# A two-layer graph kernel: exponentials with a constant scale and a bias tile, a fourteenth pair weighted on GpSimd, and a re-ordered way into the main loop

## The chip, the cores and the metric

The kernel runs on one core of one Trainium2 chip. The metric is the time of one execution on the device in microseconds (us). Three runs of the kernel before gave 10816.57, 10823.91 and 10828.75 us, so the median is 10823.91 us.

## The reference

There are 3327 nodes with 128 features, a 0/1 adjacency matrix `adj` of 3327 x 3327, and two residual layers.

```python
# layer 0
h   = relu(layernorm(x))
deg = adj.sum(axis=1); deg[deg == 0] = 1
agg = adj.T @ h / deg
x   = x + relu(batchnorm(agg @ W_n.T + b_n + h @ W_c.T + b_c))
# layer 1: 128 independent attentions of 3327 x 3327, each with 8 columns
h = relu(layernorm(x))
q, k, v = (h @ W.T).reshape(128, 3327, 8) for W in (Wq, Wk, Wv)
a = softmax(q @ k.T / sqrt(128) + adj + adj, axis=2)
x = x + (a @ v).reshape(3327, 1024) @ Wo.T
```

Nearly all of the work is the middle of layer 1: 128 score matrices of 3327 x 3327, each of which is formed, has the adjacency added twice, goes through an exponential and is multiplied by `v` with a column of ones appended, which gives the softmax's sums.

## The kernel before, in words

**Scores and their exponentials.** `HALF` is half of 1/sqrt(128), so exp(q.k/sqrt(128) + 2 adj) = exp(2 (HALF q.k + adj)). The score is kept transposed: its 3327 rows, padded to 3328, are split into 26 chunks (`NC`) of 128 partitions, and its columns into 7 blocks of 512 (`NB`), the last of 255. Four of the 128 attentions (`G`) are handled together, which gives 32 groups (`NG`); two of them make a "half". A *pair* is one chunk and one half: a tile of 128 x 2 x 512 scores, held in two PSUM banks. A block of one group has 26 x 2 = 52 pairs.

**The main loop** (`attention`, lines 592 to 794) is written out: 32 groups x 7 blocks x 13 steps (`SU`), 2912 steps of four pairs each. Three of the four are *plain*: TensorE forms the score (`product`, L662), VectorE adds the adjacency into one third of the tile `d` (`add`, L753), and ScalarE later takes one exponential of all three, 128 x 3072, in place (`late`, L781). The fourth is *weighted*: ScalarE takes the exponential straight from PSUM into the tile `f` (L761), and GpSimd multiplies it by exp(2 adj), which was worked out beforehand and lies in the DRAM tensor `wd` (L762). Pairs 0 to 38 of a block are plain and 39 to 51 weighted, so the weighted ones touch chunks 19 to 25 (`WC` = 19). TensorE then multiplies each exponential by `v` into the accumulator `av` (`weigh`, L546).

**Order.** The scheduler is off, so each engine runs its instructions in the order in which the program writes them. Step x writes: the weighted product, its exponential and its multiplication; `late`, the exponential of `d` of step x-1; plain product 0 and its add; `second(0)`, the first four `av` matmuls of step x-2 (`LAG` = 2); one part of `finish`; `beside`, one part of a projection or of an output; plain products 1 and 2 with their adds; `second(1)`, the other four `av` matmuls. Products share three PSUM tiles in turn (pool `psc`), and every step uses four. `finish` divides a block's accumulator by its sums: a VectorE copy (L554) in step 2 of the next block, four transposes (L561) in step 3, reciprocal and multiplication on VectorE (L567, L569) in step 4, a store in step 5. `beside` runs the projections that later groups need in steps 6 to 11.

**Ahead of the loop.** Layer 0 loads `x` and its weights, normalises, and passes the 26 row chunks of `adj` (tile `a`, three buffers, loads at L396) through seven PSUM accumulators (L398). After that come the degree scaling (`spread`), the two small matmuls and the batch norm (`hidden`, L446 to L457), and a bound on the largest exponent (L463 to L485), which yields `flag` and the tile `scales`. If the bound is too large, `scales` is zero, so that nothing overflows, and a slow branch redoes layer 1. `weigh_early` (L422) takes the exponentials of three adjacency blocks for `wd`; the fourth and later ones are made inside the loop (L686). Layer 1's norm goes chunk group by chunk group: `relu`, `residual`, `stats`, `second_norm` (a normalise on ScalarE), `columns` (transpose and copy). `project_now` makes the projections of the first two groups, `loads` fetches the first group's q, k and v, and a sort on GpSimd (L175) puts k in order.

Of the kernel before, what the change touches and what calls it, by code (L numbers as in the profile page):

```python
# [20 lines left out]
H = 8  # L21
# [10 lines left out]
WC = 3 * SU // 2  # L32
# [12 lines left out]
def tile_two_layer_gnn(  # L45
# [60 lines left out]
    scales = const.tile([P, 2], F32, name="scales")  # L106
# [31 lines left out]
    def loads(tiles, d):  # L138
# [12 lines left out]
        qs = [dma(*a) for b in range(G) for a in q_loads(q, 32 * b, batch(b))]  # L151
# [9 lines left out]
        for half in range(2):  # L161

# [7 lines left out]
            todo += [qs.pop(0) for _ in range(2)]  # L170
            for c in range(0, NC, 4):
                n = min(4, NC - c)

                def sort(ks=ks, c=c, n=n, half=half):
                    nc.gpsimd.tensor_copy(  # L175
                        k[:, c : c + n, half * 64 : half * 64 + 64],
                        ks.bitcast(F32).rearrange("g (p c) -> g c p", c=NC)[:, c : c + n, :],
                    )

                todo.append(sort)  # L180
                if qs:
                    todo.append(qs.pop(0))
# [90 lines left out]
    with tc.tile_pool(name="l0", bufs=1) as l0, tc.tile_pool(  # L273
# [21 lines left out]
        for c0, c1 in ((0, 8), (8, NC - 1)):  # L295
            nc.sync.dma_start(xs[:, c0:c1, :], xr[:, c0:c1, :])
# [18 lines left out]
        def stats(i):  # L315
# [5 lines left out]
            cs = slice(4 * i, min(NC, 4 * i + 4))  # L321
            nc.scalar.activation(sd[:, cs], mv[:, cs, 1], AF.Sqrt, bias=eps)

        def normalise(i, dst):

            cs = slice(4 * i, min(NC, 4 * i + 4))
            nc.vector.reciprocal(rs[:, cs], sd[:, cs])
            nc.vector.scalar_tensor_tensor(
                mr[:, cs], mv[:, cs, 0], -1.0, rs[:, cs], ALU.mult, ALU.mult
            )  # L330
# [91 lines left out]
        def weigh_early():  # L422
            a7, n0, w = weights.pop(0)
            nc.scalar.activation(a7[:, :, :w], a7[:, :, :w], AF.Exp, scale=scales[:, 0:1])
            nc.sync.dma_start(
                wd[:, :, n0 : n0 + w].rearrange("c p n -> p c n"), a7[:, :, :w]
            )

# [13 lines left out]
        for i, (n0, w) in enumerate(blocks):  # L442
            if i == NQ - 1:
                spread(i)
# [3 lines left out]
            if i >= 1:  # L448
                hidden(i - 1)
        hidden(NQ - 1)  # L450
        nc.vector.bn_aggr(bmv, bst.rearrange("p i s -> p (i s)"))
        nc.scalar.activation(scale, bmv[:, 1:2], AF.Sqrt, bias=eps)
# [5 lines left out]

        top = l0.tile([P, 1], F32, name="top")
        nc.vector.tensor_reduce(top, amax, AX.X, ALU.max)  # L463
        nc.tensor.transpose(aside[:1, :P], top, ident)
        bound = l0.tile([1, 2], F32, name="bound")
        big = l0.tile([1, 2], F32, name="big")
        for i in range(2):
            nc.vector.tensor_tensor(
                big[:, i : i + 1], norm[:, 2 * i : 2 * i + 1], norm[:, 2 * i + 1 : 2 * i + 2],
                ALU.max,  # L470
            )
        nc.vector.tensor_tensor(bound[:, 1:2], big[:, 0:1], big[:, 1:2], ALU.mult)
        nc.vector.tensor_scalar(
            bound[:, 1:2], bound[:, 1:2], (1.001 * D * H * HALF) ** 2, 1e10,
            ALU.mult, ALU.min,
        )
        nc.scalar.activation(bound[:, 1:2], bound[:, 1:2], AF.Sqrt)
        nc.vector.tensor_reduce(bound[:, 0:1], aside[:1, :P], AX.X, ALU.max)
        nc.vector.tensor_tensor(bound[:, 0:1], bound[:, 0:1], bound[:, 1:2], ALU.add)
        nc.vector.tensor_scalar(bound[:, 0:1], bound[:, 0:1], SAFE / 2, None, ALU.is_le)  # L480
        nc.vector.tensor_scalar(flag, bound[:, 0:1], -1.0, 1.0, ALU.mult, ALU.add)
        for i, f in enumerate((2.0, 2.0 * HALF)):
            nc.vector.tensor_scalar(big[:, i : i + 1], bound[:, 0:1], f, None, ALU.mult)
        nc.tensor.matmul(aside[:, :2], ones[:1, :P], big, start=True, stop=True)
        nc.vector.tensor_copy(scales, aside[:, :2])  # L485

        weigh_early()
# [13 lines left out]
        def second_norm(i):  # L501
            normalise(i, C)

        def columns(i):
            pt, cs = turned(i, C, acc[i])
            (nc.vector.tensor_copy if i % 2 else nc.scalar.copy)(B[:, cs, :], pt)
            nc.sync.dma_start(hd[:, 4 * i * P : (4 * i + pt.shape[1]) * P], B[:, cs, :])

        wk = sp
# [3 lines left out]
        def project_now(j, banks):  # L513
            todo = projections(wk, B2[:, j * CH : (j + 1) * CH], j, True, ov0)
# [6 lines left out]
        for i in range(NQ):  # L521
            relu(i)
            residual(i)
            stats(i)
            if i >= 1:
                second_norm(i - 1)
                columns(i - 1)
            if i == 1:
                project_now(0, [acc[j] for j in (2, 3, 4, 5, 6)] + [aside])
                first = loads(sets[0], 0)  # L530
                for start in first[:13]:
                    start()
                weigh_early()
            if i == 3:
                for start in first[13:]:
                    start()
        second_norm(NQ - 1)
        columns(NQ - 1)
# [12 lines left out]
    def finish(rp, av, d0, n0, w):  # L551
# [15 lines left out]
        nc.vector.reciprocal(ri[:R, :, :J], pv[:R, :, :J, H])  # L567
# [24 lines left out]
    def attention():  # L592


        with tc.tile_pool(name="adj", bufs=4) as ap, tc.tile_pool(
# [17 lines left out]
            if True:  # L613
# [8 lines left out]
                def pairs(s):  # L622

                    three = [(j // 2, j % 2) for j in range(3 * s, 3 * s + 3)]
                    j = 3 * SU + s
# [363 lines left out]
```

## Time and profile before

| | |
|---|---|
| median of three runs | 10823.91 us |
| the profiled execution: time, span of its instructions | 10826.13 us, 10824.3 us |
| granted TensorE clock over the execution | 0.994 of full |
| adjacency pass of layer 0, first to last matmul | 20.6 to 187.0 us |
| first exponential of the main loop | 291.1 us |
| end of the last exponential of the main loop | 10803.2 us |
| DMA: bytes moved, mean rate | 1786.09 MB, 165 GB/s |

Busy time is the time in which an engine executes, whatever its rate. A group of instructions is given by line, engine, operation and tiles, with its count, busy time and the mean duration of one, and then the idle time of the engine just before them with what ended it. Successive instructions of an engine may overlap, so durations can add up to more than busy time. In the timeline each row has its start, its length and its count, and in brackets the idle time before it.

### The profile page before, as it was taken

What the parts mean: (1) busy time and instruction counts of PE and PEld (TensorE: products, weight loads), DVE (VectorE), ACT (ScalarE), POOL (GpSimd) and SP (SyncE); (2) the same over time, 40 slices, a digit from 0 to 9 for tenths busy, and PEclk for the clock granted to TensorE, in tenths of its full rate; (3) what the DMA queues carried; (4) which work ended last, traced back from release to release, by engine and by line L of the source; (5) the groups of instructions that cost most, each with busy time, mean ns of one, the idle gap of its engine ahead of it and who ended that gap; (6) DMA issues with size and microseconds to landing.
All of it is one profiled execution on the core that took longest, in us unless ns stands there. A gap on an engine that the chain in (4) does not pass through costs nothing. (4 is left out here: it accounts for less than half of the span.)

```text
span 10824.3 us, 186291 instructions
## 1 busy us (share of the span) xinstructions
PE 9805.0 (91%) x72399; PEld 2707.2 (25%) x72399; DVE 9915.9 (92%) x9936; ACT 10472.1 (97%) x6009; POOL 7001.0 (65%) x3640
## 2 busy tenths in 40 slices
PE   7899999999999999999999999999999999999998
PEld 3222222222222222222222222222222222222222
DVE  5899999999999999999999999999999999999998
ACT  5999999999999999999999999999999999999999
POOL 1566666666666666666666666666666666666665
PEclk8999999999999999999999999999999999999999
DMA  7655555555555555555555555555555555555554
GB/s 243 211 170 160 162 160 168 164 163 161 159 160 171 164 161 161 160 165 167 163 162 162 160 167 163 165 162 159 158 171 163 162 162 157 163 169 162 158 153 127
DMA packets 1145405, 1786.09 MB, mean 165 GB/s; under 512 B 198430, under 2 KB 446236, under 8 KB 1137084
## 3 DMA queue, kind: packets, MB, share of 16 engines
q1 hardware_dynamic: 1141982, 1771.79, 54.2%
q8 instruction: 568, 9.31, 0.4%
q14 instruction: 329, 2.70, 0.1%
q10 hardware_dynamic: 2494, 2.30, 0.1%
q0 software_dynamic: 32, 0.00, 0.0%
HBM read 1673.22 MB, written 100.53 MB: 164 GB/s over the span
## 5 line engine op out<-in xcount | busy, mean ns | idle before, releaser
L753 DVE SCALAR_TENSOR_TENSOR d<-s,at 128x1024 f32<-128x1024 f32 x8736 | 9454.2, 1141 | 746.9 <-PE s L662 711.5
L762 POOL TENSOR_TENSOR f<-f,wt 128x1024 f32<-128x1024 f32 x2912 | 6500.9, 2232 | 3529.7 <-ACT f L761 3526.0
L781 ACT ACTIVATE d<-d,scales 128x3072 f32<-128x3072 f32 x2912 | 7784.4, 2673 | 20.6 <-DVE d L753 1.0
L546 PE MATMUL av<-d,v 128*9 128x512 f32 x34944 | 5707.1, 565 | 560.0 <-ACT d L781 559.4
L662 PE MATMUL s<-q,k 32*128 32x512 f32 x23296 | 4106.5, 479 | 377.3 <-DVE d L753 294.0
L761 ACT ACTIVATE f<-s,scales 128x1024 f32<-128x1024 f32 x2912 | 3049.8, 1047 | 169.5 <-PE s L662 152.9
L662 PEld LDWEIGHTS s<-q,k 32*128 32x128 f32 x23296 | 1668.7, 181 | 5492.7 <-DVE d L753 3460.9
L546 PE MATMUL av<-f,v 128*9 128x512 f32 x11648 | 2834.0, 565 | 0.0
L546 PEld LDWEIGHTS av<-d,v 128*9 128x9 f32 x34944 | 653.7, 88 | 2016.2 <-ACT d L781 1223.9
L175 POOL CAST k<-ks 128x256 fp32r<-128x256 f32 (+1 forms) x448 | 286.8, 642 | 61.9 <-DMA ks<-kT 41.3
L546 PEld LDWEIGHTS av<-f,v 128*9 128x9 f32 x11648 | 307.1, 88 | 0.0
L398 PE MATMUL acc<-a,A 128*128 128x512 f32 (+1 forms) x364 | 151.7, 569 | 20.6 <-DMA a<-in_adj 20.6
L561 PEld LDWEIGHTS av<-ident,avs 128*128 128x128 f32 (+1 forms) x864 | 121.0, 208 | 179.3 <-issue 178.2
L561 PE MATMUL av<-ident,avs 128*128 128x128 f32 (+1 forms) x864 | 163.5, 310 | 0.5 <-DVE avs L554 0.5
L215 POOL TENSOR_TENSOR o<-pf,o 104x512 fp32r<-104x512 f32 x120 | 154.3, 1286 | 9.6
L554 DVE COPY avs<-av 128x512 f32<-128x512 f32 (+1 forms) x224 | 144.0, 643 | 2.8 <-PE av L546 2.8
L405 DVE TENSOR_REDUCE amax<-a 128x1 f32<-128x3327 f32 x26 | 93.7, 3611 | 40.7 <-DMA a<-in_adj 40.7
L398 PEld LDWEIGHTS acc<-a,A 128*128 128x128 f32 x364 | 69.0, 192 | 105.5 <-issue 105.3
L402 ACT ACTIVATE junk<-a 128x3327 bf16<-128x3327 f32 x26 | 77.4, 2977 | 6.7 <-DMA a<-in_adj 6.5
L213 DVE COPY pf<-av 104x512 f32<-104x512 f32 x120 | 81.7, 681 | 0.0
L371 POOL TENSOR_TENSOR sq<-wk 128x512 f32<-128x512 f32 x2 | 2.1, 1040 | 112.6 <-PE aside L372 112.6
L214 POOL CAST o<-pf 104x512 fp32r<-104x512 f32 x120 | 73.6, 614 | 0.0
(107 smaller groups left out, 899.8 us busy)
## 6 DMA issues: line engine op xcount, KB each, us to landing
at<-in_adjT SPq DMA_DIRECT2D x1920, 512.0 KB
wt<-wd SPq DMA_DIRECT2D x1344, 256.0 KB
at<-in_adjT SPq DMA_DIRECT2D x320, 255.0 KB
ks<-kT SPq DMA_DIRECT2D x512, 104.0 KB
q<-qT SPq DMA_DIRECT2D x512, 104.0 KB
a<-in_adj SPq DMA_DIRECT2D x26, 1663.5 KB
wt<-wd SPq DMA_DIRECT2D x224, 127.5 KB
qT<-o SPq DMA_DIRECT2D x128, 208.0 KB
```

The costliest lines, as they stand in the source:

```text
L175: nc.gpsimd.tensor_copy(k[:, c : c + n, half * 64 : half * 64 + 64], ks.bitcast(F32).rearrange("g (p c) -> g c p", c=NC)[:, c : c + n, :],)
L215: nc.gpsimd.tensor_tensor(o[:CH, 1], f[:CH], o[:CH, 0].bitcast(F32), ALU.subtract)
L398: nc.tensor.matmul(acc[i][:, :w], A[:, c, :], a[:, n0 : n0 + w], start=(c == 0), stop=(c == NC - 1),)
L405: nc.vector.tensor_reduce(amax[:, c : c + 1], a[:, :N], AX.X, ALU.max, apply_absolute_value=True)
L546: nc.tensor.matmul(av[32 * b : 32 * b + H + 1, :w], tiles[2][:, b, c, :], e, start=first, stop=last,)
L554: nc.vector.tensor_copy(avs[:, :w], av[:, :w])
L561: nc.tensor.transpose(pt[:R, j, :], avs[:, j : j + (R - 1) * J + 1 : J], ident)
L662: nc.tensor.matmul(p[:, x, :we], k[rs, c, :], q[rs, n0 : n0 + we], start=True, stop=True,)
L753: nc.vector.scalar_tensor_tensor(d[:, j, :, :w], p[:, :, :w], HALF, have[0, i, y, c // 2][:, c % 2, :w] .unsqueeze(1).to_broadcast([P, 2, w]),
L761: nc.scalar.activation(f[:, :, :w], p[:, :, :w], AF.Exp, scale=scales[:, 1:2])
L762: nc.gpsimd.tensor_tensor(f[:, :, :w], f[:, :, :w], have[1, i, y, ps[3][0]][:, :w].unsqueeze(1).to_broadcast([P, 2, w]), ALU.mult,)
L781: nc.scalar.activation(flat, flat, AF.Exp, scale=scales[:, 0:1])
```

## The change

Six things are done.

1. All exponentials take `scale=2.0` (or `2.0 * HALF`) as a constant and the tile `low` as a bias, where before they took `scales` as a scale and no bias. `low` is 0 when the bound holds and -1e30 otherwise. The bound is worked out without a square root, and ahead of the batch norm.
2. Step 12 of every block has two plain and two weighted pairs, so pairs 0 to 37 are plain and 14 are weighted. `WC` stays 19; the last adjacency tile of a block is loaded with one chunk instead of two.
3. `finish` takes the maximum of the sums and 1e-30 ahead of the reciprocal.
4. `x` is loaded from ScalarE's queue instead of SP's, so the first adjacency loads lead SP's queue.
5. Two of the three `weigh_early` calls move to the batch norm's loop; the last group's `spread` moves ahead of it.
6. Layer 1's norm: chunk group 0 by itself, then one square root, one reciprocal and one product for all others; normalise on VectorE and GpSimd instead of ScalarE; the relu in `columns`; one store of `hd`. The first group's q loads go out from ScalarE's queue, ahead of the rest, all loads at once, and three of every seven sorts of k run on VectorE.

```diff
-WC = 3 * SU // 2
+WC = 19
...
-            nc.sync.dma_start(xs[:, c0:c1, :], xr[:, c0:c1, :])
+            nc.scalar.dma_start(xs[:, c0:c1, :], xr[:, c0:c1, :])
...
-            nc.scalar.activation(a7[:, :, :w], a7[:, :, :w], AF.Exp, scale=scales[:, 0:1])
+            nc.scalar.activation(a7[:, :, :w], a7[:, :, :w], AF.Exp, bias=low, scale=2.0)
...
-            if i == NQ - 1:
-                spread(i)
             s = slice(n0, n0 + w)
             nc.vector.tensor_tensor(B2[:, s], acc[i][:, :w], B2[:, s], ALU.mult)
             nc.tensor.matmul(acc[i][:, :w], wn, B2[:, s], start=True, stop=True)
             if i >= 1:
                 hidden(i - 1)
+            if i in (3, 6):
+                weigh_early()
...
-        for i in range(NQ):
-            relu(i)
-            residual(i)
-            stats(i)
-            if i >= 1:
-                second_norm(i - 1)
-                columns(i - 1)
-            if i == 1:
-                project_now(0, [acc[j] for j in (2, 3, 4, 5, 6)] + [aside])
-                first = loads(sets[0], 0)
-                for start in first[:13]:
-                    start()
-                weigh_early()
-            if i == 3:
-                for start in first[13:]:
-                    start()
-        second_norm(NQ - 1)
-        columns(NQ - 1)
+        relu(0)
+        residual(0)
+        relu(1)
+        stats(0, False)
+        relu(2)
+        roots(0, 4)
+        residual(1)
+        factors(0, 4)
+        second_norm(0, nc.vector)
+        columns(0, True)
+        relu(3)
+        stats(1, False)
+        residual(2)
+        project_now(0, [acc[j] for j in (6, 5, 4, 0)] + [aside, acc[1]])
+        first = loads(sets[0], 0, True)
+        for start in first:
+            start()
+        for i in range(4, NQ):
+            relu(i)
+        for i in range(2, NQ):
+            if i > 2:
+                residual(i)
+            stats(i, False)
+        roots(4, NC)
+        factors(4, NC)
+        for i in range(1, NQ):
+            second_norm(i, nc.gpsimd if i % 3 == 0 else nc.vector)
+        for i in range(1, NQ):
+            columns(i, i % 2 == 0)
+        keep_columns(0, NQ)
         project_now(1, [acc[j] for j in (0, 1, 2, 3, 4, 5)])
         weigh_early()
...
-        nc.vector.reciprocal(ri[:R, :, :J], pv[:R, :, :J, H])
+
+        nc.vector.tensor_scalar(ri[:R, :, :J], pv[:R, :, :J, H], 1e-30, None, ALU.max)
+        nc.vector.reciprocal(ri[:R, :, :J], ri[:R, :, :J])
...
-                    three = [(j // 2, j % 2) for j in range(3 * s, 3 * s + 3)]
-                    j = 3 * SU + s
-                    return three + [(j // 2, j % 2)]
+
+                    last = s == SU - 1
+                    plain = [(j // 2, j % 2) for j in range(3 * s, 3 * s + 3 - last)]
+                    rest = [(WC + s // 2, 1 - s % 2)]
+                    return plain, rest + ([(NC - 1, 0)] if last else [])
...
-                    p = product(i, y, *ps[3])
-                    nc.scalar.activation(f[:, :, :w], p[:, :, :w], AF.Exp, scale=scales[:, 1:2])
...
+                    def weighted(c, half):
+                        f = fp.tile([P, 2, NB], F32, name="f")
+                        p = product(i, y, c, half)
+                        nc.scalar.activation(
+                            f[:, :, :w], p[:, :, :w], AF.Exp, bias=low, scale=2.0 * HALF
+                        )
+                        nc.gpsimd.tensor_tensor(
+                            f[:, :, :w], f[:, :, :w],
+                            have[1, i, y, c][:, :w].unsqueeze(1).to_broadcast([P, 2, w]),
+                            ALU.mult,
+                        )
+                        es.append(f)
+
+                    weighted(*rest[0])
                     if late is not None:
                         late()
-                    add(0, product(i, y, *ps[0]))
+                    add(0, product(i, y, *plain[0]))
                     if due:
                         second(0)
                     step()
                     beside(i, y, s)
-                    add(1, product(i, y, *ps[1]))
-                    add(2, product(i, y, *ps[2]))
+                    add(1, product(i, y, *plain[1]))
+                    if len(rest) > 1:
+                        weighted(*rest[1])
+                    else:
+                        add(2, product(i, y, *plain[2]))
...
-                        nc.scalar.activation(flat, flat, AF.Exp, scale=scales[:, 0:1])
+                    def late(d=d, w=w, n=len(plain)):
+                        flat = d[:, :n].rearrange("p j x n -> p (j x) n")[:, :, :w]
+                        nc.scalar.activation(flat, flat, AF.Exp, bias=low, scale=2.0)
```

## The prediction

> **What bounds the kernel now.** I read the busy table first, then ScalarE's groups by shape, then the waits, then single steps of the timeline.
>
> The page's busy table (busy us, share of the span, instructions):
>
> ```profile
> span 10824.3 us, 186291 instructions
> PE 9805.0 (91%) x72399; PEld 2707.2 (25%) x72399; DVE 9915.9 (92%) x9936; ACT 10472.1 (97%) x6009; POOL 7001.0 (65%) x3640
> ```
>
> ScalarE (ACT) leads, and most of its idle time is not in the loop. The same by stages (ahead of the loop, the loop, after it; columns: length, then busy us and count of PE, PEld, DVE, ACT, POOL):
>
> ```profile
> 212.00:291.00 79.00, 34.45 (x82) 15.45 (x82) 25.04 (x90) 35.41 (x58) 9.02 (x17) 0.59 0.75 218
> 291.00:10803.00 10512.00, 9587.74 (x71831) 2605.56 (x71831) 9764.08 (x9678) 10328.08 (x5840) 6970.92 (x3587) 1.00 0.54 163
> ```
>
> In the loop ScalarE is idle for 10512 - 10328 = 184 us of 10512: it sets the pace. Its groups by shape (busy us, mean ns of one, idle before):
>
> ```profile
> L781 ACT ACTIVATE d<-d,scales 128x3072 f32<-128x3072 f32 x2496 | 7133.0, 2858 | 19.9 <-DVE d L753 0.3
> L761 ACT ACTIVATE f<-s,scales 128x1024 f32<-128x1024 f32 x2496 | 2763.3, 1107 | 123.6 <-PE s L662 107.2 <-POOL k L175 7.3 <-issue 6.8
> L781 ACT ACTIVATE d<-d,scales 128x1530 f32<-128x1530 f32 x416 | 651.4, 1566 | 0.7 <-DVE d L753 0.7
> L761 ACT ACTIVATE f<-s,scales 128x510 f32<-128x510 f32 x416 | 286.5, 689 | 45.8 <-PE s L662 45.7
> ...
> L364 ACT ACTIVATE C<-aside,bias 128x512 f32<-128x512 f32 x6 | 4.1, 688 | 17.1 <-PE aside L361 17.1
> ...
> L452 ACT ACTIVATE bn_scale<-bn_mv,eps 128x1 f32<-128x1 f32 x1 | 0.3, 294 | 3.1 <-DVE bn_mv L451 3.1
> L477 ACT ACTIVATE bound<-bound 1x1 f32<-1x1 f32 x1 | 0.2, 202 | 1.4 <-DVE bound L473 1.4
> ```
>
> Successive exponentials overlap: over the 2496 full steps, the median from the start of `f` to that of `d` is 1.00 us and from `d` to the next `f` 2.75 us, so an undisturbed step takes 3.74 us. VectorE's three adds take 3.49 us (below): it follows closely, and is late where it has more to do. That is step 4 of a block, where `finish` divides; here are ScalarE's and VectorE's timelines in one such step (start, length):
>
> ```profile
> 361.00 2.85 ACT L781 ACTIVATE d<-d,scales 128x3072 f32<-128x3072 f32 x1
> 363.75 1.10 ACT L761 ACTIVATE f<-s,scales 128x1024 f32<-128x1024 f32 x1
> 364.85 2.86 ACT L781 ACTIVATE d<-d,scales 128x3072 f32<-128x3072 f32 x1
> ```
>
> ```profile
> 358.51 3.49 DVE L753 SCALAR_TENSOR_TENSOR d<-s,at 128x1024 f32<-128x1024 f32 x3 [0.70 <-PE s L662]
> 361.92 0.25 DVE L567 RECIPROCAL ri<-av 128x16 f32<-128x16 f32 x1
> 362.20 0.29 DVE L569 TENSOR_TENSOR oq<-av,ri 128x128 f32<-128x128 f32 x1
> ```
>
> The last `d` starts at the end of `f` (364.85), not 0.10 us ahead of it. Over the 150 full blocks that follow a full one (from the third group on), the `d` of step 4 starts 93 to 94 ns after the step's third add, from the 5th to the 95th percentile; in steps 0 and 1 it starts some 0.71 us after it. So in step 4 VectorE sets ScalarE's pace.
>
> **1. Constant scale, bias tile: 0.** What matters is how many per-partition operands an exponential reads. Without one, the 1x1 square root L477 took 202 ns; with a bias tile, L452 took 294: an operand costs 92 ns. Before, each exponential has a scale tile; after, a bias tile. From PSUM, L364 with a bias tile took 688 ns for 512 columns, L761 with a scale tile 689 for 510: equal within 3 ns. 5,824 of them at 3 ns would be 17 us; I take 0. If the tile were free: -5,824 x 92 ns = -536 us, and ScalarE's step of 3.74 - 0.18 = 3.56 us would still be longer than VectorE's 3.49, so that is the lower end.
>
> **2. The fourteenth pair: +32 us.** ScalarE's elements stay the same, but step 12 has three exponentials instead of two. `d` of 3072 becomes 2048: the slope between its two forms is (2858 - 1566)/(3072 - 1530) = 0.838 ns, so 0.858 us go. A second `f` comes, 1.00 us from start to start. Net +0.14 us x 192 full blocks = 27; short blocks 0.589 - 0.427 = +0.16 x 32 = 5. VectorE loses 224 adds (1.16 us each between starts), GpSimd gains 224 multiplications of 2.39 us:
>
> ```profile
> L762 POOL TENSOR_TENSOR f<-f,wt 128x1024 f32<-128x1024 f32 x2496 | 5967.4, 2391 | 3146.9 <-ACT f L761 3143.1 <-DMA wt<-wd 3.7
> ```
>
> GpSimd waits 3147 us for `f`, and the result is used two steps later, so its added 0.5 ms is hidden; if that cover failed, 224 x 2.39 = 535 us. VectorE's gap in step 12 brings nothing, I think: its lead is bounded by the three PSUM tiles, and by the products behind `second`, which waits for ScalarE's `d`. In steps 0 and 1 it is already 0.71 us ahead, and the losses come later: in step 3 TensorE's four transposes hold the adds up again. Bounds: 10 (a short block's steps are partly TensorE's) to 45.
>
> The Trainium skill (GPSIMD Engine Reference, section 4.1) speaks against the move: two-input elementwise work is about 2x slower on GpSimd than on VectorE. The rows agree on the rate (2391 against 1217 ns) but show a waiting GpSimd; by the rule, with 1.17 us more on the path of 224 blocks, the sum would be 262 us higher.
>
> **3. The maximum in `finish`: +42 us.** One VectorE instruction on 128x16 from PSUM, like the reciprocal it precedes (0.25 us, 0.28 to the next start); the reciprocal then reads SBUF and waits for it, like the 128x4 ones at 0.16 us, so 0.17 and 0.21 to the next start. Step 4 has 0.28 + 0.21 - 0.28 = 0.20 us more. VectorE being last there, it passes through to `d`: 160 blocks, 32 short ones (also 94 ns) and about half of the 31 first blocks of a group, some 208 x 0.20 = 42. What is queued behind it on VectorE is adds 1 and 2 of that step; who waits is `d`. Bounds: 0 (a lead from step 12 reaches step 4) to 60 (0.27 us each, as for a second PSUM read).
>
> **4. Adjacency first: +4 us.** The adjacency pass is TensorE's (busy 164.9 of 166.4 us), so only its start at 20.6 us counts. Before, ScalarE had its first chunk of `A` at 14.4 us and the pass waited for `a`. Now two `a` loads run beside `x`, which comes later than 10 us; ScalarE's queue issues the other loads in order, and in the built program some of those issues wait for the landing of `x` and of both `a`. `x`, `a`, `a` are 5.1 MB; at the 283 GB/s of the first 20 us they land at 18 to 20 us; four more issues at 0.4 us, table load 1.3, square root 0.5, factors 1.1 make 23 to 26. At 400 GB/s it would be 19. Bounds -3 to +15.
>
> **5. Bound and early exponentials moved: -3 us.** They leave the path behind the batch norm (208.3 to 211.5 us), but the bound and the last `spread` now stand ahead of the first B product in VectorE's and TensorE's queues (187.2 becomes about 192). The relu that starts layer 1 moves from 211.5 to about 208.5. Two of six activation table loads go, 1.30 us each here (231.67 to 232.97). By the Trainium skill (ScalarE: Activation LUTs, section "What ACT_TABLE_LOAD costs") a switch is about 2.66 us with its drain; no such drain stands in this trace; by the page two more us or so would go.
>
> **6. Layer 1's norm: -1 us.** ScalarE loses 22 normalises of 0.4 us and six square roots, but its queue now holds 16 q issues (about 0.6 us each where seven stood on SP), some waiting for earlier transfers, ahead of relu 4 to 6. VectorE's sorts of k's second half stand ahead of `stats(2)`; they wait for loads that can only start when the first half's buffer is sorted, about 12 us in all (before, first sort 242.3, second half landed 267.0). Counted through, VectorE is free at about 247 to 250 instead of stepping along; 8 us of residuals and stats, 9 of normalise and columns follow: `columns` ends at 264 to 268 against 269.5. From there the path is as before: project, exponential, its store must land (290.9), loop. Bounds -20 to +20.
>
> **Sum:** 0 + 32 + 42 + 4 - 3 - 1 = +74 on the profiled execution's 10826.1, less some 5 for short blocks in which TensorE, not ScalarE, is last: 10895. The profiled execution lies 2.2 above the median: **10893 us, 0.64% slower**.
>
> **Rivals.** A measurement here can tell about 0.2% (22 us) from no change.
> - *The bias tile is cheaper than the scale tile* (the other side). Place: 5,824 exponentials; price up to 92 ns each; above 12 ns each it outweighs the +69 and from 16 ns the kernel is faster by over 0.2%. At full price 10893 - 536 = 10357, or somewhat more, as VectorE's 3.49 us then leaves little room. Against it: 688 and 689 ns. Chance 8%.
> - *Step 12's free VectorE time carries into steps 2 to 5.* Then the maximum costs nothing and part of the 39 us that steps 3 and 5 of full blocks now take beyond 3.74 us each comes back: 10893 - 42 - (0 to 39) = 10812 to 10851. For it: 1.16 us freed. Against: the 0.71 us bound. Chance 20%.
> - *The way in gets longer*: ScalarE blocked on q issues, VectorE on sorts: +25, 10920. Chance 14%. *Or shorter* by 25: 10868. Chance 12%.
> - Forecast (10875 to 10910): 43%. Something else: 3%.
>
> Faster: 8%, the lower end of the second rival 4, other 2: 14%. Same: the rest of that rival's lower half and the lowest shorter way in, 16%. Slower: 70%. The range 10805 to 10945 takes in the second rival and both ways in; it leaves out the cheap tile and tails.
>
> **What would show it.** Right: `d` and `f` keep their durations (2858, 1107) with `low`; `d` of 2048 takes about 2.0 us; step 12 plus step 0 last 0.14 us longer; `d` of step 4 starts 94 ns after its add and 0.2 us later; the loop, 291 to 10803 before, is 60 to 80 us longer. Wrong: shorter exponentials; or slack at step 4; or a first `f` 20 us off 291.

## The result, and the profile after

The changed kernel takes 10925.59 us (median of four runs, 10920.39 to 10928.46), the kernel before 10823.62 in four runs beside it: a ratio of 1.0094, 95% interval 1.0077 to 1.0112. So it is 0.94% slower, by 102 us. The prediction was 10893 us (slower, 70%) with a range of 10805 to 10945. The profiled execution took 10925.71 us, its span is 10924.0 us, 99.7 longer than before.

The page's busy table (busy us, share of the span, instructions):

```profile
span 10924.0 us, 186996 instructions
...
PE 9819.1 (90%) x72399; PEld 2713.0 (25%) x72399; DVE 9738.8 (89%) x9955; ACT 10492.5 (96%) x6201; POOL 7481.9 (68%) x3864
```

VectorE has 177 us less work than before, GpSimd 481 more, ScalarE 20 more. The same by stages, ahead of the loop and in it (length, then busy us and count of PE, PEld, DVE, ACT, POOL; then clock, DMA share, GB/s):

```profile
212.00:298.70 86.70, 24.50 (x82) 14.63 (x82) 32.12 (x106) 16.98 (x23) 9.99 (x17) 0.60 0.64 160
298.70:10902.50 10603.80, 9611.36 (x71831) 2611.97 (x71831) 9580.15 (x9677) 10363.21 (x6064) 7450.44 (x3811) 1.00 0.53 157
```

The loop took 10512 us before and takes 10604, and ScalarE's idle time in it rose from 184 to 241 us. The stretch from 212 us to the loop went from 79 to 86.7 us. ScalarE's groups by shape (busy us, mean ns of one, idle before):

```profile
L832 ACT ACTIVATE d<-d,low 128x3072 f32<-128x3072 f32 x2304 | 6587.3, 2859 | 50.6 <-DVE d L794 31.2
L804 ACT ACTIVATE f<-s,low 128x1024 f32<-128x1024 f32 x2688 | 2967.9, 1111 | 144.6 <-PE s L703 130.0 <-POOL k L181 7.9 <-DMA wd<-a 6.7
L832 ACT ACTIVATE d<-d,low 128x1530 f32<-128x1530 f32 x384 | 601.5, 1566 | 6.2 <-DVE d L794 6.2
L832 ACT ACTIVATE d<-d,low 128x2048 f32<-128x2048 f32 x192 | 386.8, 2015 | 0.0
```

The durations with a bias tile are those with a scale tile (2858, 1107, 1566), and the `d` of two pairs takes 2015 ns. What is new is the end of the first line: `d` waits for VectorE's adds, 31.2 us in all against 0.3. That is step 4 of a block. ScalarE and VectorE there, in the block that the prediction showed (start, length):

```profile
369.17 2.85 ACT L832 ACTIVATE d<-d,low 128x3072 f32<-128x3072 f32 x1
371.92 1.10 ACT L804 ACTIVATE f<-s,low 128x1024 f32<-128x1024 f32 x1
373.22 2.86 ACT L832 ACTIVATE d<-d,low 128x3072 f32<-128x3072 f32 x1 [0.20 <-DVE d L794]
```

```profile
370.09 0.16 DVE L604 TENSOR_SCALAR ri<-av 128x16 f32<-128x16 f32 x1
370.29 0.25 DVE L605 RECIPROCAL ri<-ri 128x16 f32<-128x16 f32 x1
370.57 0.29 DVE L607 TENSOR_TENSOR oq<-av,ri 128x128 f32<-128x128 f32 x1
370.78 6.87 DVE L794 SCALAR_TENSOR_TENSOR d<-s,at 128x1024 f32<-128x1024 f32 x6
```

Before, the `d` of this step started at the end of its `f`; now it starts 0.20 us after it, and three small instructions stand ahead of the adds where there were two.

To see where the 99.7 us are, I took from both traces the time from each step's first `f` to the next step's and summed the differences by the place of the step in its block:

| where | us | prediction |
|---|---|---|
| full blocks: step 12 and the step after it | +27.2 | +27 |
| short blocks: step 12 and the step after it | +12.2 | +5, less 5 |
| step 5, where step 4's late `d` is felt | +40.7 | +42 |
| step 2 of full blocks, nearly all of it in the first block of a group | +10.6 | nothing |
| first exponential of the loop, 291.14 to 298.74 | +7.6 | 0 (+4, -3, -1) |
| all else | +1.4 | |

Step 2 of the first block was in no sum. In group 0 it is long in both kernels; of the other 31 groups it is about 0.9 us longer than the usual 3.74 in 18, against 4 before. The first two lines below are steps 1 and 2 of group 8 in the changed kernel, the last two the same steps of group 10 (the third number from the end is the granted clock):

```profile
2965.06:2968.82 3.76, 3.04 (x26) 0.93 (x24) 3.76 (x4) 3.76 (x3) 3.45 (x2) 1.00 0.55 155
2968.82:2973.48 4.66, 4.51 (x28) 0.88 (x32) 3.54 (x5) 3.85 (x3) 2.38 (x1) 0.63 0.23 79
3627.67:3631.43 3.76, 3.06 (x26) 0.94 (x24) 3.76 (x4) 3.76 (x3) 3.45 (x2) 1.00 0.59 190
3631.43:3635.18 3.75, 3.30 (x24) 0.81 (x24) 3.75 (x5) 3.75 (x4) 2.40 (x1) 1.00 0.25 88
```

The two groups run the same instructions. In group 8 the granted clock falls to 0.63 in that one step (the trace's clock records hold one stretch at half the clock there, 3.41 us from 2968.93), the first twelve matmuls into `av` take 0.98 to 1.06 us instead of 0.60, and TensorE, busy for 4.51 of 4.66 us, is the last for once.

### The profile page after: what moved, and what is told of

Read it like the earlier page. It is cut to its first block, busy times and chain, and to the rows that moved or that the text cites. A ratio compares the mean times of both kernels' runs of the same rounds, so it can differ in the third digit from the quotient of the medians.

```text
span 10924.0 us, 186996 instructions
## 1 busy us (share of the span) xinstructions
PE 9819.1 (90%) x72399; PEld 2713.0 (25%) x72399; DVE 9738.8 (89%) x9955; ACT 10492.5 (96%) x6201; POOL 7481.9 (68%) x3864
## 3 DMA queue, kind: packets, MB, share of 16 engines
q14 instruction: 333, 2.73, 0.1%
## 5 line engine op out<-in xcount | busy, mean ns | idle before, releaser
L794 DVE SCALAR_TENSOR_TENSOR d<-s,at 128x1024 f32<-128x1024 f32 x8512 | 9230.2, 1139 | 1014.4 <-PE s L703 981.1
L807 POOL TENSOR_TENSOR f<-f,wt 128x1024 f32<-128x1024 f32 (+1 forms) x3136 | 6983.1, 2233 | 3143.7 <-ACT f L804 3136.3
L832 ACT ACTIVATE d<-d,low 128x3072 f32<-128x3072 f32 (+1 forms) x2912 | 7612.5, 2614 | 56.8 <-DVE d L794 37.4
L582 PE MATMUL av<-d,v 128*9 128x512 f32 x34048 | 5506.2, 567 | 597.6 <-ACT d L832 596.2
L804 ACT ACTIVATE f<-s,low 128x1024 f32<-128x1024 f32 (+1 forms) x3136 | 3269.3, 1051 | 190.4 <-PE s L703 175.7
L582 PEld LDWEIGHTS av<-d,v 128*9 128x9 f32 x34048 | 630.3, 88 | 2004.6 <-ACT d L832 1216.1
L181 POOL CAST k<-ks 128x128 fp32r<-128x128 f32 (+1 forms) x442 | 287.5, 651 | 61.1 <-DMA q<-qT 47.9
```

Source lines behind the costliest of these rows:

```text
L181: (nc.vector if alone and c % 8 else nc.gpsimd).tensor_copy(k[:, c : c + n, half * 64 : half * 64 + 64], ks.bitcast(F32).rearrange("g (p c ...
L582: nc.tensor.matmul(av[32 * b : 32 * b + H + 1, :w], tiles[2][:, b, c, :], e, start=first, stop=last,)
L794: nc.vector.scalar_tensor_tensor(d[:, j, :, :w], p[:, :, :w], HALF, have[0, i, y, c // 2][:, c % 2, :w] .unsqueeze(1).to_broadcast([P, 2, w]),
L804: nc.scalar.activation(f[:, :, :w], p[:, :, :w], AF.Exp, bias=low, scale=2.0 * HALF)
L807: nc.gpsimd.tensor_tensor(f[:, :, :w], f[:, :, :w], have[1, i, y, c][:, :w].unsqueeze(1).to_broadcast([P, 2, w]), ALU.mult,)
L832: nc.scalar.activation(flat, flat, AF.Exp, bias=low, scale=2.0)
```

## Experiments

My theory for the loop: two losses that do not touch each other, the fourteenth pair (ScalarE's own time) and the maximum (VectorE is last in step 4); and for the way in, queues that hold ScalarE and VectorE up. The rivals: VectorE's freed time does carry over, and the losses come from elsewhere. "The changed kernel" is 10925.6 us; times are medians, ratios are to the kernel before.

### Without the maximum

```diff
-        nc.vector.tensor_scalar(ri[:R, :, :J], pv[:R, :, :J, H], 1e-30, None, ALU.max)
-        nc.vector.reciprocal(ri[:R, :, :J], ri[:R, :, :J])
+        nc.vector.reciprocal(ri[:R, :, :J], pv[:R, :, :J, H])
```

> The changed kernel without the maximum in `finish`: the reciprocal reads the sums from PSUM again. Theory (VectorE is the last to arrive in step 4 of a block, so its 0.20 us more pass through): about 41 us less than the changed kernel's 10925.6, so some 10885, 0.56% above before; the period from step 4's `f` to step 5's `f` in blocks 1 to 5 goes back from 4065 to about 3867 ns, and no other step changes. Rival (VectorE has a lead in step 4, thanks to the add that step 12 no longer has, and the loss at step 5 comes from elsewhere): no difference, 10925.

Measured: 10873.5 us, ratio 1.0045 (1.0031 to 1.0059), 52 us less than the changed kernel. (The period that the expectation gives to step 4 is the one that starts with step 5's `f`, in which the `d` of step 4 stands; I call it step 5.) Step 5 of blocks 1 to 5 is back at 3862 ns, and over all blocks it gives back 35.4 + 6.1 = 41.5 us. A further 13.6 us came from somewhere that I had excluded: step 2 of full blocks, slow in the first block of 3 groups instead of 18. For the maximum the theory holds, with its number; the rival (a lead in step 4) falls.

### Thirteen weighted pairs

```diff
-                    last = s == SU - 1
-                    plain = [(j // 2, j % 2) for j in range(3 * s, 3 * s + 3 - last)]
-                    rest = [(WC + s // 2, 1 - s % 2)]
-                    return plain, rest + ([(NC - 1, 0)] if last else [])
+                    j = 3 * SU + s
+                    return [(i // 2, i % 2) for i in range(3 * s, 3 * s + 3)], [(j // 2, j % 2)]
...
-                            n = min(2, WC - 2 * c)
+                            n = 2
```

> The changed kernel with 13 weighted pairs in a block, split as before (three plain, one weighted in every step, step 12 too). Theory (an exponential of a third less and one more of PSUM cost ScalarE 0.14 us net a block): steps 12 and 0 together lose 39 us, so about 10886. If the slow step 2 in the first block of a group (17 of 32 groups in the changed kernel, 4 before, each about 0.9 us) hangs on the fourteenth pair, some 11 us more, so about 10875. Rival (the 1.16 us that VectorE is spared in each block is worth something in steps 2 to 5): the loss at step 5 grows beyond 4065 ns and less than 39 us come back.

Measured: 10875.0 us, ratio 1.0046 (1.0032 to 1.0060). Steps 12 and 0 give back 38.8 us, slow steps 2 (none left of 18) 15.5, the way in, whose code is the same, takes 3.4. In blocks 1 to 5, step 5 stands at 4068 ns against 4065: the 1.16 us that VectorE is spared in each block with 14 pairs are worth nothing in steps 2 to 5. That was the prediction's second rival (20%), and it falls here. In first blocks step 5 is longer without the fourteenth pair (3951 ns on average against 3848), but that goes with the slow step 2: in the changed kernel it takes 3765 ns in the 18 groups that have one, and 3964 in the other 13.

### Maximum in step 4, reciprocal and product in step 5

```diff
         nc.vector.tensor_scalar(ri[:R, :, :J], pv[:R, :, :J, H], 1e-30, None, ALU.max)
+        yield
         nc.vector.reciprocal(ri[:R, :, :J], ri[:R, :, :J])
```

> The changed kernel with one more yield in `finish`: the maximum in step 4, reciprocal and product in step 5, the store in step 6. Theory (a step's extra VectorE work passes through only as far as it exceeds the lead that VectorE has; in step 4 0.55 us more cost 0.12 and 0.75 us cost 0.32, so the lead is about 0.43): step 4 with 0.19 is hidden, step 5 with 0.56 loses 0.07 to 0.13; together 0.2 to 0.25 us less in some 200 blocks, 40 to 50 us, so about 10880. Rival (the lost lead only shows one step later, in step 6, which TensorE's projections already hold up, or the lead isn't there twice): no difference, or a few us.

Measured: 10863.7 us, ratio 1.0036 (1.0022 to 1.0049), 62 us less than the changed kernel. Step 5 falls to 3743 ns, an undisturbed step, which gives back 54.3 + 12.0 us; step 6 takes 5.4 of that, mostly in short blocks. So both halves are hidden whole, the second with 0.56 us too. My lead of 0.43 us was too small: it gave 0.07 to 0.13 us of loss in step 5, and there is none. The same work costs 0.32 us in one step and nothing in two: the maximum is still there, and yet this is 10 us ahead of the run without it, although step 2 of the first block is slow in 12 groups here and in 3 there.

The kernel before has the same place, with reciprocal and product alone:

```diff
         nc.vector.reciprocal(ri[:R, :, :J], pv[:R, :, :J, H])
+        yield
```

> The kernel before with one yield more in `finish`: reciprocal in step 4, product in step 5. Nothing else is changed. Theory (a step's extra VectorE work costs only what exceeds its lead of about 0.4 us): step 5's 3867 ns in full blocks falls to 3744, in the first block 3758 stays, in the short block 2271 falls to 2085: 160 x 0.123 + 31 x 0.186, about 25 us less, so 0.23% faster than before. Rival (the lead is only there because of the step's own rhythm, and the product loses as much in step 6): no difference.

Measured: 10810.2 us, ratio 0.9986 (0.9977 to 0.9995). Step 5 gives back 19.4 + 5.8 = 25.2 us and falls to 3745 ns, as the theory has it. The loop gained only 15.1, mainly since step 2 of the first block was slow in 14 groups instead of 4, which took 7.5 back. So the slow step 2 does not hang on the fourteenth pair, as the run with 13 pairs had seemed to show: it comes in a kernel with 13 as well.

### Exponentials without an operand

```diff
-                        nc.scalar.activation(flat, flat, AF.Exp, bias=low, scale=2.0)
+                        nc.scalar.activation(flat, flat, AF.Exp, scale=2.0)
```

and the same for the other exponentials. The guard against overflow is left out.

> The changed kernel with all exponentials without a per-partition operand: constant scale, no bias tile (the guard against overflow is left out). Theory (an operand costs 92 ns whatever it feeds): `d` goes from 2859 to about 2767 ns and `f` from 1111 to about 1019; 6,048 exponentials in the loop give up to 556 us, so 10370, but VectorE's three adds (3.49 us) and what `finish` and the projections add to them then set the pace in more steps, so I expect 10420 to 10530. Rival (the 92 ns belong to the small tiles on which they were measured, not to an operand): durations unchanged and no difference.

Measured: 10646.1 us, ratio 0.9834 (0.9819 to 0.9849). ScalarE's groups in this kernel:

```profile
L832 ACT ACTIVATE d<-d 128x3072 f32<-128x3072 f32 x2304 | 6387.1, 2772 | 145.8 <-DVE d L794 143.6
L804 ACT ACTIVATE f<-s 128x1024 f32<-128x1024 f32 x2688 | 2730.8, 1023 | 201.2 <-PE s L703 182.1 <-POOL k L181 11.3 <-DMA wd<-a 6.8
```

The tile costs 87 and 88 ns per exponential in these two forms, and 80 to 86 ns in the rarer ones, from 510 to 2048 elements: the 92 ns that the prediction read from two tiny square roots was right in kind and 5% too high. An undisturbed step falls from 3745 to 3560 ns, as twice the price says. But of 6,048 x 88 = 532 us only some 282 arrive in the loop, and the time lies 116 us above the top of my expectation: waits for VectorE in front of `d` grow from 31 to 144 us, those for products in front of `f` from 130 to 182, and the steps that hold projections, copies and the divide hardly move (step 5: 4065 to 4088 ns, step 8: 3838 to 3794). I take it that those were VectorE's and TensorE's steps already; for step 5 the runs above show it, for the others it is argued.

### The way in, four variants

These are read at the stage, as the whole time is that of a single execution. In the changed kernel ScalarE's and VectorE's timelines are (start, length, what ended the idle time):

```profile
227.32 32.88 ACTq L153 DMA_DIRECT2D q<-qT  x16
260.24 2.01 ACT L506 ACTIVATE A<-A,bn_shift,bn_scale 128x512 f32<-128x512 f32 x3 [32.36 <-DMA q<-qT]
```

```profile
244.86 1.98 DVE L181 CAST k<-ks 128x256 fp32r<-128x256 f32 x3 [15.07 <-DMA q<-qT]
260.90 2.04 DVE L181 CAST k<-ks 128x256 fp32r<-128x256 f32 x3 [14.05 <-DMA ks<-kT]
262.86 0.85 DVE L324 BATCH_NORM_STATS2 ln_st<-xs 128x6 f32<-128x128 f32 x4
```

Sixteen q issues hold ScalarE's queue for 32.9 us, 2 us each, and relus 4 to 6 stand behind them. VectorE waits 14 to 15 us for each half of k before it can go on to the stats. Why an issue takes 2 us here no run shows.

The q loads back on SP's queue (first and third variant):

```diff
-            (lambda a=a: nc.scalar.dma_start(*a)) if alone else dma(*a)
+            dma(*a)
...
-            if alone and half == 0:
-                todo += [qs.pop(0) for _ in range(len(qs))]
```

The sorts back on GpSimd (second and third):

```diff
-                    (nc.vector if alone and c % 8 else nc.gpsimd).tensor_copy(
+                    nc.gpsimd.tensor_copy(
```

x back on SP's queue (fourth):

```diff
-            nc.scalar.dma_start(xs[:, c0:c1, :], xr[:, c0:c1, :])
+            nc.sync.dma_start(xs[:, c0:c1, :], xr[:, c0:c1, :])
```

> The changed kernel with the first group's q loads back on SP's queue, between the sorts of k, as before; the sorts stay on VectorE and GpSimd. Read at the way in, not in the whole time. Theory (two waits lie side by side: ScalarE's relus 4 to 6 wait behind 16 q issues until 260, VectorE's stats behind the sorts of k's second half until 263): relus 4 to 6 run by about 232, but VectorE is still held by the sorts, whose second half lands when the first is sorted plus 16 to 20 us; layer 1's columns end at 265 to 272 instead of 277 to 281, first exponential of the loop 288 to 294 instead of 299 to 302. Rival (ScalarE's queue alone is the cause): columns end by 255.

> The changed kernel with all sorts of k on GpSimd, the q loads on ScalarE's queue as changed. Theory (two waits side by side): VectorE is free by 230, but its residual 4 needs relu 4, which stands behind the q issues until 260 to 262; columns end at 275 to 282, first exponential of the loop 297 to 303, no change. Rival (VectorE's sorts alone are the cause): columns end by 255.

> Both undone: q loads on SP's queue between the sorts, all sorts on GpSimd. Theory: relus 4 to 6 at about 230, stats and residuals by 245; GpSimd's two chunk groups of the normalise now stand behind its sorts (end about 265), so columns still end at 262 to 270, and the first exponential comes at 286 to 292, some 10 us ahead of the changed kernel. Rival (the loads themselves are late, whoever waits for them): columns end at 275 or later.

> The changed kernel with x loaded from SP's queue again, ahead of the adjacency. Theory (the two adjacency loads and x share the DMA engines, and ScalarE's issues wait for x): the first matmul of the adjacency pass comes at 20.6 instead of 23.3 and the pass ends at about 187.5 instead of 190.3; relu 0 of layer 1 then at about 209.3 instead of 212.1. Rival (the pass is held up by something else, for instance by the bias or the weights' loads): first matmul stays at 23.

| us | before | changed | q on SP | sorts on GpSimd | both | x on SP |
|---|---|---|---|---|---|---|
| adjacency pass, first matmul | 20.61 | 23.35 | 23.09 | 23.45 | 23.57 | 21.59 |
| adjacency pass, end | 187.16 | 190.32 | 190.14 | 190.61 | 190.64 | 188.25 |
| first relu of layer 1 | 211.45 | 212.02 | 211.86 | 212.33 | 212.34 | 209.96 |
| last relu ends | 261.97 | 262.25 | 229.33 | 262.26 | 229.89 | 260.29 |
| last `columns` ends | 269.55 | 277.21 | 276.88 | 273.85 | 265.17 | 276.87 |
| first exponential of the loop | 291.14 | 298.74 | 298.38 | 295.55 | 287.21 | 298.57 |
| whole time | 10826.6 | 10925.6 | 10928.5 | 10920.3 | 10916.1 | 10926.8 |

How far do such stage times scatter? The runs without the maximum, with 13 pairs and with the spread divide have the same way in as the changed kernel, and their first exponential comes at 299.73, 302.18 and 301.75 us; the kernel before with its divide split has it at 289.98. So one trace places the first exponential to 1 to 3.5 us, and the way in is longer by something between 7.6 and 12.2 us.

Undone alone, the q loads free ScalarE by 33 us and bring nothing that stands out of this scatter (0.4 us): VectorE still waits 29.2 us in two sorts. I had expected 265 to 272 for `columns`; k's second half landed no earlier. Undone alone, the sorts free VectorE, which then waits 29.6 us for a residual whose relu is still behind the q issues; 3.2 us come back, where I had expected none, and that is at the edge of the scatter. Undone together they bring 11.5 us, clear of it, and as much as was lost. Then VectorE runs through, until it waits for GpSimd:

```profile
229.81 0.86 DVE L322 BATCH_NORM_STATS2 ln_st<-xs 128x6 f32<-128x128 f32 x4
...
244.58 0.68 DVE L526 TENSOR_SCALAR B<-acc 128x512 f32<-128x512 f32 x1
262.77 0.69 DVE L526 TENSOR_SCALAR B<-acc 128x512 f32<-128x512 f32 x1 [17.51 <-PE acc L351]
...
256.45 4.03 POOL L179 CAST k<-ks 128x256 fp32r<-128x256 f32 x7 [13.94 <-DMA q<-qT]
260.48 2.58 POOL L516 TENSOR_SCALAR C<-xs,ln_rs,ln_mr 128x128 f32<-128x128 f32 x6
```

The last 17.5 us of waiting are for the two chunk groups of the normalise that stand behind GpSimd's sorts. So the theory of two waits side by side holds, and both single-cause rivals fall.

The x loads: on SP's queue the adjacency pass starts 1.8 us earlier and ends 2.1 us earlier, and so does the first relu, but the first exponential gains 0.2, which is nothing beside the scatter; VectorE still waits for k in between. About two of the 2.7 us are explained; the scatter of this start between runs of unchanged code is about 1 us (19.49 and 20.61 in two kernels with the same head).

### Put together

A version that keeps the guard: 13 pairs, the spread divide, q loads and sorts as in the third variant above, all of layer 1's normalise on VectorE, and the third early exponential ahead of the second group's projections:

```diff
-        second_norm(i, nc.gpsimd if i % 3 == 0 else nc.vector)
+        second_norm(i, nc.vector)
...
+        weigh_early()
         keep_columns(0, NQ)
         project_now(1, [acc[j] for j in (0, 1, 2, 3, 4, 5)])
-        weigh_early()
```

> A version that keeps the guard: the changed kernel with 13 weighted pairs; the maximum in step 4 and reciprocal with product in step 5; q loads on SP's queue between the sorts, sorts on GpSimd, all of layer 1's normalise on VectorE and the third early exponential ahead of the second group's projections. Theory (the losses add up from where they were measured): the loop of the run with 13 pairs, 10547 us, less the 60 to 65 that the spread divide gave back, so 10482 to 10490, and a first exponential at 276 to 282: about 10782 in all (10775 to 10795), 0.4% below before. Rival (the spread divide only gains where step 12 spares VectorE an add): the loop stays above 10500 and the time above 10800.

Measured: 10816.4 us, ratio 0.9991 (0.9982 to 1.0000), hardly ahead of before and 34 us over what I expected. The divide gave back its 63 us (69.3 in step 5, less 6.2 in step 6). Slow steps 2 (5 groups, against none in the run with 13 pairs) took back 6.4, and some 8 us more are spread over other steps. The two numbers of the rival, a loop above 10500 us (10502.6) and a time above 10800, thus came true, but not its mechanism: step 5 falls to 3742 ns here too, with 13 pairs. The way in failed: `columns` end at 248.09, 29 us earlier, and the first exponential still comes at 293.48 instead of 276 to 282. SP's queue and, in the last line, ScalarE (start, length):

```profile
244.57 12.14 SPq L147 DMA_DIRECT2D ks<-kT  x8
257.05 4.20 SPq L147 DMA_DIRECT2D q<-qT  x7
261.78 5.08 SPq L509 DMA_DIRECT2D xd<-xs  x4
268.06 1.14 SPq L434 DMA_DIRECT2D wd<-a  x1
269.62 3.56 SPq L530 DMA_DIRECT2D hd<-B  x1
273.27 7.16 SPq L225 DMA_DIRECT2D qT<-o  x4
...
285.28 0.58 ACT L213 CAST o<-acc 104x512 fp32r<-104x512 f32 x1 [32.48 <-DMA qT<-o]
```

The loads for the first group hold the queue until 261 us; stores that are ready at 250 are issued at 268 to 280, and ScalarE waits 32.5 us for a buffer that one of them must empty. So, as I read the timeline, from 250 us on no engine's work holds the loop up, but the order of SP's queue does; no run moved the stores to test it. I had moved work and not its transfers.

Without the guard and without the maximum, and with reciprocal and product in steps 4 and 5, with 14 pairs and with 13:

> No per-partition operand, no maximum (the guard against overflow is left out), reciprocal in step 4 and product in step 5, 14 weighted pairs, the way in as in the guarded version. Theory: of the run without an operand (10646), step 5's 4088 ns against an undisturbed 3560 falls by about two thirds and the first exponential comes 20 to 24 us earlier: 10540 to 10570. Rival (VectorE and TensorE now have no lead at all, so the loss is pushed on to steps 6 and 8): 10600 or more.

> The same with 13 weighted pairs. Theory (without the operand ScalarE's step is 3.56 us and VectorE's three adds 3.49, so an add that VectorE is spared has a worth that it had not with the operand): slower than with 14 pairs, by 10 to 60 us, the opposite of what the pair did in the changed kernel. Rival (ScalarE still sets the pace, step 12 costs it 0.05 to 0.14 us a block more with 14 pairs): faster than with 14 by 10 to 40 us.

Measured: 10534.0 us, ratio 0.9729 (0.9714 to 0.9744), with 14; 10529.1 us, 0.9727 (0.9712 to 0.9742), with 13. The first is 6 us under the range that the theory gave: the spread divide without the maximum brought 111 us (step 5 from 4088 to 3561 ns), not two thirds of the loss but all of it. The way in fell short again (first exponential at 290.42 and 287.53, against 301.70 in the run without an operand, where 20 to 24 us were expected). The second run is 5 us faster than the first. The theory falls, as 13 pairs are not slower: the VectorE time that the pair frees still bought nothing. The rival's place is right and its size at its lowest: ScalarE's loss in steps 12 and 0 fell to 10.6 us with the shorter exponentials, and part of that was made up by slow steps in the first blocks (step 2 slow in 3 groups with 14 pairs, in 8 with 13). Both are 2.7% faster than the kernel before. Of the 392 us between the changed kernel and the first, the operand alone had brought 279.

## Why the prediction came out as it did

The side was right and the time 33 us short, of 102. It lies above the narrow forecast (10875 to 10910) and inside the range. The two large terms, the fourteenth pair and the maximum, were right in place and size; the rest is three smaller losses that the sum had at nothing.

- **Constant scale and bias tile, 0:** right. 2859 and 1111 ns against 2858 and 1107. The first rival (a cheaper bias tile, 8%) fell.
- **Fourteenth pair, 32:** 27.2 in full blocks, as worked out. Failed: "short blocks 0.589 - 0.427 = +0.16 x 32 = 5", and "less some 5 for short blocks in which TensorE, not ScalarE, is last". The extra `f` made short step 12 0.39 us longer, and nothing came back: the step after a short block lasts 2.748 us with `d` of 1530 or of 1020 elements. In group 8 of the changed kernel (columns as in the stages above) VectorE is busy throughout it and ScalarE for 2.15 us of 2.75:

```profile
2962.31:2965.06 2.75, 2.33 (x28) 0.85 (x24) 2.75 (x3) 2.15 (x4) 2.56 (x2) 1.00 0.98 327
```

  So ScalarE's shorter `d` met a step that was not ScalarE's; 12.2 us where the sum had 0. I had seen that short steps are not ScalarE's and counted it as relief, while it takes away only what the change gives back. GpSimd took its 224 multiplications without a loss, as its row shows:

```profile
L807 POOL TENSOR_TENSOR f<-f,wt 128x1024 f32<-128x1024 f32 x2688 | 6412.9, 2391 | 2843.1 <-ACT f L804 2835.7 <-DMA wt<-wd 3.6
```

  It still waits 2836 us for `f`. The Trainium skill (GPSIMD Engine Reference, section 4.1) has two-input elementwise work about 2x slower on GpSimd than on VectorE, and the rows agree (2391 against 1215 ns); but the pair cost 39 us, and not the 262 that the prediction worked out from that rule, as GpSimd's result is not needed at once.
- **Maximum, 42:** 40.7. The parts were off and compensate, which is luck: maximum 163 ns and reciprocal from SBUF 253, not about 250 and 170. "About half" of the first blocks was luck too: there the maximum costs 0.20 us in the 13 groups without the slow step 2 and nothing in the other 18. `d` of step 4 starts 94 ns after its add, before and after.
- **Adjacency first, +4, and bound moved, -3:** the first matmul came 2.7 us later and the first relu of layer 1 0.6 later; their sum was to be +1. Right, as far as one trace tells: with the same way in as before, the run with the split divide has its first matmul at 19.49 and its first relu at 209.35, 1.1 and 2.1 us earlier.
- **Layer 1's norm, -1:** failed. "VectorE is free at about 247 to 250" became 262.9, and "`columns` ends at 264 to 268" became 277.2. The term that was too small is the loads: 16 q issues at an estimate of 0.6 us took 2.06 us each, and the k loads let VectorE into its two sorts only at 245 and 261, where I had counted 12 us for both halves together. The third rival (a longer way in, +25, 14%) thus came true by a third, 7.6 us in the profiled pair, beside the forecast.
- **The clock:** in no sum, 10.6 us.

Of the 33 us, 12.2 short blocks, 10.6 clock, 7.6 way in, less 1.3 for the maximum, make 29; the rest is 1.4 in other steps and the distance between medians and profiled executions.

**Which groups the clock hits.** The slow step 2 of the first block was seen in 18, 19, 19, 20 and 11 of 31 groups in five kernels with the same loop, in 12 with the spread divide, in 3 without the maximum, in 4 and 3 with 14 pairs and no operand, and in 0, 4, 5, 8 and 14 in the kernels with 13 pairs. So it does not belong to one edit. The traces show what decides between groups. Their clock records start on a grid of 3.41 us, which holds to 0.02 us through a whole execution. In the five kernels with the same loop, all 87 slow groups start step 1 of the first block 2.73 to 3.31 us after a point of this grid, and none of the other 68 does. In the four kernels with 13 pairs and an operand, it is 2.39 to 3.01 us for all 23, and for none of the other 101. So the count changes with whatever shifts the groups against the grid, the way in included. Open: what in TensorE's work just before makes the clock fall. At about 0.9 us each these steps are worth up to 18 us, as much as the smallest effects here, and a verdict on 0.1% in this kernel has to count them first.

## What to carry to other kernels

Where two engines run close together, a small instruction on the follower costs its whole duration if it stands in the step in which the follower is already late, and nothing in the next: look for the place before you look for a cheaper instruction. Time freed on the follower is worth nothing in steps that the leader sets, and time freed on the leader is worth nothing in steps that it does not set: here half of what the operand cost stayed behind in such steps. When two waits end at the same time, taking away either shows little; undo them together, and then read the queue that issues the transfers. Before a stage's time is read from one trace, look it up in other runs that left that stage alone: here the same code placed the first exponential up to 3.5 us apart.

## What the runs showed of the hardware

- A per-partition bias tile of an exponential costs 87 to 88 ns in the two commonest forms (128x3072 and 128x1024), 80 to 86 in the others. With a scale tile and no bias the same two forms take 2858 and 1107 ns, with a constant scale and the bias tile 2859 and 1111, so the one is as dear as the other within 4 ns. The Trainium skill (ScalarE: Activation LUTs, section "What ACT_TABLE_LOAD costs") gives about 93 ns for such an operand; the two forms agree within 6 ns.
- The same section gives 2.66 us for a table switch with its drain. In the changed kernel a cast ends at 287.49 us, the load starts at 287.50 and takes 1.28, and the exponential starts at 288.80: 1.31 us in all, and the same between the neighbours of the switches at 197.68 and 205.44.
- The granted clock can fall to 0.63 for one step in a loop in which TensorE is busy for 81% of the step before. A loss of 0.37 of 4.66 us is 1.72 us of clock, or 3.4 us at half rate, as the clock record there has it (3.41 us at 0.5). The Trainium skill (TensorE: Matmul & The Clock Gate, Part 1) tells of a free-running window of 3.4 us and a half rate after an idle one. The length, the half rate and the fixed grid fit; the idle window does not stand in this trace, where TensorE's longest gap around it is 0.49 us.
- Sixteen loads of 104 KB from ScalarE's queue took 2.06 us each to issue while SP's queue loaded k; on SP's queue, between the sorts, they took 0.45 to 0.68 us each (first and third variant).
